# The last pair of row tiles: one finished earlier and normalized by ScalarE, the other's last product in two pieces, with bn_stats, stored by halves

## The chip, the cores and the metric

The kernel runs on one core of a Trainium2 chip. The core has a matrix engine (TensorE, PE in the profile; its weight loads are PEld), a vector engine (VectorE, DVE), an activation engine (ScalarE, ACT), a general engine (GpSimd, POOL), and SyncE (SP), which here issues nearly all transfers between the chip's memory (HBM) and the core's SBUF. Matrix products go to PSUM, from where VectorE or ScalarE fetch them. The metric is the device time of one execution in microseconds (us). The engines run in parallel and wait for each other through semaphores.

## The reference

All arrays are float32. x has 4 x 512 rows of 1024. The two layers, cut to what matters:

```python
attn = einsum('ds,td->st', w1, w2) * sparse_mask          # (1024, 1024), a band
y    = gelu(einsum('bds,st->bdt', x, attn) + b2)          # exact gelu
x    = layernorm(x + y)                                   # eps 1e-5, over 1024
w_l  = table lookup of 4-bit codes; w_h = of 8-bit codes  # (1024, 1024) each
y    = where(norm(x) > 64, x @ w_h.T, x @ w_l.T) + bias
x    = layernorm(x + y)
```

The kernel computes with a banded mask and with w_l alone, counts the rows and mask columns for which that isn't enough, and branches at the end to a general path if there are any. There are none with these inputs, so the general path is jumped over.

## The kernel before

Rows are taken in NT = 16 row tiles of P = 128 rows; D = 1024, HALF = 512, KT = 8 blocks of 128 along the contraction, EARLY = 4, PAIR = 2. The first layer and the unpacking of the codes come first; the second layer follows. w_l.T + I stands in SBUF as wT (the I adds the residual x). Row tiles 0 to 3 have the second layer by plain products (`ffn_half`). Row tiles 4 to 15 have it in six pairs (`ffn_pair(pool, n, blocks, between)`), by a scheme that needs seven products of half size instead of eight: the two row tiles' inputs in halves of the contraction are a11, a12 (row tile n) and a21, a22 (row tile n+1), their sums and differences are s1 to s4, the weight's quarters are b11, b12, b21, b22, and differences of them t1 to t4. The seven products of a pair go into three PSUM buffers of 512 columns, u, v and w; each is a call of `times`, which makes four matmuls of 128 x 512, and a float32 matmul shows as two instructions in the profile, so eight per product. In the program's order:

- u = a11*b11; DVE writes y11 = u + bias (line 642)
- w = s1*t1; y22 = w + bias (line 646)
- u += s2*t2; y12 = u + bias (line 649)
- w += s4*b22; row tile n's right half is w + y12 (line 651)
- u += s3*t3; row tile n+1's right half is u + y22 (line 653)
- v = a12*b21; row tile n's left half is v + y11 (line 656), and row tile n is finished
- u += a22*t4; row tile n+1's left half is u + bias (line 659), and row tile n+1 is finished

`combine` (line 522) is the addition on DVE that writes the result into x_tiles and sums it over its columns into `sums`. `finish_rows` (line 534) adds the two sums (line 537), and `stats` (line 347) makes the negative mean (line 351), lets ACT square and sum the centred row (line 354), and POOL turn that into one over the standard deviation r (lines 356 and 357). The last step, `normalize` on DVE (line 361) and the store by SP (line 546), is put on a list, `later`, which `now()` works off: for row tile n after the pair's last `combine` (line 660), for row tile n+1 in the next pair (line 643), or, in the last pair, at line 759.

DVE executes in the order in which the program is written (line 715). The other engines' order is made by a planner from the program's order and an estimate of the time: in the last pair it put the first half of v's eight matmuls ahead of s2*t2, and the other half behind s3*t3. POOL prepares s2 and s4 of a pair (lines 615 and 616). SP's transfers inside the pairs (lines 583, 589) reorder the next pair's rows; the last pair has none. After the pairs every engine loads the count of exceptions (line 762), and branches (line 763). At the end SP passes a row of semaphores and all engines meet in a barrier (line 798).

The buffers that the change touches: `work` tag "z" (two buffers, outputs o of row tiles from 4 on), `last` tag "o" (outputs of row tiles 0 to 3), `b2_bc` (the first layer's bias in all partitions, last read in the first layer), `bias_bc`.

Of the kernel before, what the change touches and what calls it, by code (L numbers as in the profile page):

```python
# [9 lines left out]
FP = mybir.dt.float32  # L10
# [3 lines left out]
AF = mybir.ActivationFunctionType  # L14
ALU = mybir.AluOpType
AX = mybir.AxisListType

P = 128
D = 1024
SOON = 12  # L20
PAIR = 2
KT = D // P
HALF = 512
NH = D // HALF
EPS = 1e-5
# [167 lines left out]
def kernel(  # L193
# [13 lines left out]
    nc = tc.nc  # L207
    x = x.flatten_outer_dims()
    out = out.flatten_outer_dims()
    NT = x.shape[0] // P  # L210
# [4 lines left out]
    with ExitStack() as main:  # L215
# [9 lines left out]
        work = main.enter_context(tc.tile_pool(name="work", bufs=1))  # L225
# [21 lines left out]
        minus_half = const.tile([P, 1], FP, name="minus_half")  # L247
# [3 lines left out]
        b2_bc = const.tile([P, D], FP, name="b2_bc")  # L251
        bias_bc = const.tile([P, D], FP, name="bias_bc")
# [94 lines left out]
        def stats(u, total):  # L347


            nm = work.tile([P, 1], FP, tag="nm", name="nm", bufs=4)  # L350
            nc.vector.tensor_scalar(nm, total, -1.0 / D, None, ALU.mult)  # L351
            junk = work.tile([P, D], BF, tag="junk", name="junk", bufs=1)
            ss = work.tile([P, 1], FP, tag="ss", name="ss", bufs=4)
            nc.scalar.activation(junk, u, AF.Square, bias=nm, accum_out=ss)  # L354
            r = work.tile([P, 1], FP, tag="r", name="r", bufs=4)
            nc.gpsimd.tensor_scalar(r, ss, 1.0 / D, EPS, ALU.mult, ALU.add)  # L356
            nc.gpsimd.tensor_tensor(r, r, minus_half, ALU.pow)  # L357
            return nm, r, ss

        def normalize(dst, u, nm, r):  # L360
            nc.vector.tensor_scalar(dst, u, nm, r, ALU.add, ALU.mult)  # L361

        x_tiles = []
# [9 lines left out]
        with tc.tile_pool(name="prod", bufs=1) as prod:  # L373
# [41 lines left out]
            for s in range(KT):  # L415
# [4 lines left out]
                for k in range(KT):  # L420
                    nc.tensor.matmul(  # L421
                        out=ps[:, : hi - lo],
                        lhsT=w1_sb[s][:, k, :],
                        rhs=w2T[:, k, lo:hi],
                        start=(k == 0),
                        stop=(k == KT - 1),
# [55 lines left out]
        def now():  # L482
            while later:
                later.pop(0)()
# [35 lines left out]
        sums = const.tile([P, NT, NH], FP, name="sums")  # L520

        def combine(n, h, ps, other):

            return nc.vector.scalar_tensor_tensor(  # L524
                x_tiles[n][:, ts(h, HALF)],
                ps,
                1.0,
                other,
                ALU.mult,
                ALU.add,  # L530
                accum_out=sums[:, n, h : h + 1],
            )

        def finish_rows(n):
            y = x_tiles[n]
            total = work.tile([P, 1], FP, tag="total", name="total", bufs=4)
            nc.vector.tensor_tensor(total, sums[:, n, 0:1], sums[:, n, 1:2], ALU.add)
            nm, r, _ = stats(y, total)

            def rest():  # L540
                if n < EARLY:
                    o = last.tile([P, D], FP, tag="o", name="o")
                else:
                    o = work.tile([P, D], FP, tag="z", name="o", bufs=2)
                normalize(o, y, nm, r)
                nc.sync.dma_start(out=out[ts(n, P), :], in_=o)

            later.append(rest)
# [14 lines left out]
        b21, b22 = wT[:, KH:, :HALF], wT[:, KH:, HALF:]  # L563
# [55 lines left out]
        def ffn_pair(pool, n, blocks, between):  # L619

            a11, a12, a22, s1, s2, s3, s4 = blocks
            t1, t2, t3, t4 = (weights[i] for i in range(1, 5))
            u = pool.tile([P, HALF], FP, tag="u", name="u", bufs=2)
            v = pool.tile([P, HALF], FP, tag="v", name="v", bufs=1)
            w = pool.tile([P, HALF], FP, tag="w", name="w", bufs=1)

            def times(ps, a, b, start, stop):
                for k in range(KH):
                    nc.tensor.matmul(  # L629
                        out=ps,  # L630
                        lhsT=a[:, k, :],
                        rhs=b[:, k, :],
                        start=start and k == 0,
                        stop=stop and k == KH - 1,
                        skip_group_check=True,
                    )

            left, right = bias_bc[:, :HALF], bias_bc[:, HALF:]
            y11, y12 = x_tiles[n][:, :HALF], x_tiles[n][:, HALF:]
            y22 = x_tiles[n + 1][:, HALF:]  # L640
            times(u, a11, b11, True, False)
            nc.vector.tensor_tensor(y11, u, left, ALU.add)
            now()
            between(0)
            times(w, s1, t1, True, False)
            nc.vector.tensor_tensor(y22, w, right, ALU.add)
            between(1)
            times(u, s2, t2, False, False)
            nc.vector.tensor_tensor(y12, u, right, ALU.add)  # L649
            times(w, s4, b22, False, True)  # L650
            combine(n, 1, w, y12)
            times(u, s3, t3, False, False)
            combine(n + 1, 1, u, y22)
            between(2)
            times(v, a12, b21, True, True)
            combine(n, 0, v, y11)
            finish_rows(n)
            times(u, a22, t4, False, True)
            combine(n + 1, 0, u, left)
            now()  # L660
            finish_rows(n + 1)

        def count_odd():


            nc.vector.tensor_scalar(ssq, ssq, EST_T * EST_T, None, ALU.is_gt)
            nc.vector.tensor_scalar(outside, outside, 0.0, None, ALU.is_equal)
            nc.vector.tensor_scalar(outside, outside, -1.0, 1.0, ALU.mult, ALU.add)
            n_odd = const.tile([P, 1], FP, name="n_odd")
            nc.vector.tensor_reduce(n_odd, odd, AX.X, ALU.add)  # L670
            return n_odd
# [39 lines left out]
        for i, (what, n) in enumerate(todo):  # L711
# [4 lines left out]
            if (what, n) == ("attention", SOON - 2):  # L716
# [3 lines left out]
                last = main.enter_context(tc.tile_pool(name="last", bufs=1, side="right"))  # L720
# [32 lines left out]
        for n in range(EARLY, NT, PAIR):  # L753
            ffn_pair(ps_pair, n, blocks[n], lambda part, m=n + PAIR: prepare_pair(m, part))
            if n == EARLY:
                n_odd = count_odd()
            elif n == EARLY + PAIR:
                count_all(n_odd)
# [44 lines left out]
```

## Time and profile before

| what | us |
|---|---|
| median of three runs (366.29 to 367.3) | 366.83 |
| the profiled execution | 366.59 |
| its span, first to last instruction | 364.7 |
| TensorE busy in the span | 328.5 (90%) |
| VectorE busy | 231.1 (63%) |
| ScalarE busy | 166.3 (46%) |
| GpSimd busy | 83.5 (23%) |
| last product of the last pair on TensorE | 350.02 to 353.62 |
| start of the last normalization on VectorE | 357.71 |
| issue of the last store by SyncE | 358.55 |

The mean granted TensorE clock of this execution is 0.966 of full speed. Times inside the execution count from the start of its span. A row of the profile names the line, the engine, the operation, what it writes and reads with the shapes, and how often; a "q" behind an engine's name (SPq, ACTq) means the engine's instruction queue, which waits, branches and issues transfers while the engine itself may still be busy. A span's end is not its time: 1.9 us of the profiled execution lie outside its span.

### The profile page before, as it was taken

How to read it: one execution, taken by the hardware profiler on the slowest of the kernel's cores; microseconds unless marked ns; L12 is line 12 of the kernel's file. 1: busy time of each engine (PE TensorE's matmuls, PEld its weight loads, DVE VectorE, ACT ScalarE, POOL GpSimd, SP SyncE). 2: the span in 40 equal slices, each digit the busy share in tenths (PEclk: the TensorE clock that was granted, in tenths of full speed). 3: DMA queues.
4: the chain of work that ended last, by engine and by line, in shares of the span. 5: the costliest groups of instructions: out<-in, count | busy, mean ns of one | idle time of the engine just before them, and what ended most of it. 6: DMA issues, size and time to landing. Idle time of an engine off the chain costs nothing.

```text
span 364.7 us, 3670 instructions
## 1 busy us (share of the span) xinstructions
PE 328.5 (90%) x1202; PEld 202.1 (55%) x1202; DVE 231.1 (63%) x351; ACT 166.3 (46%) x242; POOL 83.5 (23%) x130
## 2 busy tenths in 40 slices
PE   4599977989999997999999888999999999999970
PEld 3488866876566586866665433443444444444430
DVE  2589887887988997367676854564635526634130
ACT  0994983989649975675444411301212112012011
POOL 0600420454054111212312440401203004013000
PEclk9699998999999999699999999999999999999995
DMA  9997407700011000812154315143251451432003
GB/s 224 333 373 238 162 2 290 286 2 0 3 46 43 0 3 6 309 44 100 39 176 158 120 58 173 58 177 112 115 180 50 175 170 58 173 117 115 1 4 121
DMA packets 28347, 43.90 MB, mean 120 GB/s; under 512 B 7584, under 2 KB 20640, under 8 KB 28320
## 3 DMA queue, kind: packets, MB, share of 16 engines
q1 hardware_dynamic: 23056, 43.00, 33.3%
q10 hardware_dynamic: 5264, 0.59, 1.2%
q8 instruction: 11, 0.18, 0.2%
q14 instruction: 16, 0.13, 0.1%
HBM read 28.90 MB, written 14.68 MB: 119 GB/s over the span
## 4 chain that ended last, share of the span: by engine, by line
PE 34%; DVE 27%; ACT 16%; issue 8%; DMA 6%; POOL 5%; SPq 1%; ACTq 1%; POOLq 0%; DVEq 0%
PE u L629 16%; PE w L629 8%; ACT junk L354 7%; DVE x L498 5%; PE v L629 4%; DMA rows<-there 3%; DVE e L310 3%; PE mm L467 3%; ACT e L303 3%; DVE z L493 3%; POOL r L357 2%; POOL r L356 2%; DVE root L312 2%; DVE root L311 2%; ACT z L494 2%
## 5 line engine op out<-in xcount | busy, mean ns | idle before, releaser
L354 ACT ACTIVATE junk<-x,nm 128x1024 bf16<-128x1024 f32 x32 | 36.8, 1148 | 66.2 <-DVE nm L351 63.9
L467 PE MATMUL mm<-attn,xT 128*128 128x198 f32 (+2 forms) x320 | 63.7, 357 | 3.0 <-ACT xT L264 3.0
L467 PEld LDWEIGHTS mm<-attn,xT 128*128 128x128 f32 x320 | 55.6, 200 | 10.4 <-ACT xT L264 3.2
L303 ACT ACTIVATE e<-v,lt,diff 128x1024 f32<-128x1024 uint8 x48 | 56.7, 1238 | 6.1 <-DVE v L278 6.1
L512 PE MATMUL mm<-wT,xT 128*128 128x512 f32 x128 | 56.5, 594 | 0.6 <-DVE x L524 0.6
L629 PE MATMUL u<-t,halves 128*128 128x512 f32 x96 | 43.3, 594 | 1.0 <-DVE x L649 1.0
L356 POOL TENSOR_SCALAR r<-ss 128x1 f32<-128x1 f32 x32 | 11.5, 359 | 123.9 <-ACT junk L354 123.9
L512 PEld LDWEIGHTS mm<-wT,xT 128*128 128x128 f32 x128 | 23.7, 190 | 27.7 <-issue 27.4
L307 POOL TENSOR_SCALAR root<-v,diff,lt 128x1024 f32<-128x1024 uint8 x16 | 24.3, 1524 | 58.6 <-DVE v L278 44.0
L629 PEld LDWEIGHTS u<-t,halves 128*128 128x128 f32 x96 | 18.1, 190 | 24.6 <-issue 22.8
L611 ACT COPY halves<-rows 128x1024 f32<-128x1024 f32 x6 | 6.3, 1042 | 55.6 <-DMA rows<-there 55.6
L579 DVE STREAM_TRANSPOSE squares<-x 128x1024 f32<-128x1024 f32 x12 | 24.3, 2026 | 11.5 <-DMA there<-squares 11.5
L421 PE MATMUL mm<-w2T,w_sb 128*128 128x268 f32 (+1 forms) x128 | 30.0, 391 | 0.0
L615 POOL TENSOR_TENSOR halves<-halves 128x512 f32<-128x512 f32 x6 | 9.5, 1584 | 85.4 <-DVE halves L612 85.4
L263 PE MATMUL pt<-ident,x 128*128 128x128 f32 x160 | 22.4, 284 | 7.0 <-ACT wT L264 6.4
L421 PEld LDWEIGHTS mm<-w2T,w_sb 128*128 128x128 f32 x128 | 24.9, 203 | 3.1
L361 DVE TENSOR_SCALAR x<-x,nm,r 128x1024 f32<-128x1024 f32 x16 | 13.0, 812 | 20.4 <-POOL r L357 15.8
L311 DVE COPY_PREDICATED root<-v,e 128x1024 f32<-128x1024 uint8 x16 | 22.5, 1405 | 5.3 <-ACT e L303 4.0
L264 ACT COPY xT<-pt 128x512 f32<-128x512 f32 x40 | 21.0, 585 | 10.3 <-PE pt L263 7.2
L498 DVE SCALAR_TENSOR_TENSOR x<-z,x 128x1024 f32<-128x1024 f32 x16 | 21.5, 1342 | 5.3 <-ACT z L494 5.3
L263 PEld LDWEIGHTS pt<-ident,x 128*128 128x128 f32 x160 | 19.2, 155 | 10.0 <-ACT wT L264 7.8
L494 ACT ACTIVATE z<-z 128x1024 f32<-128x1024 f32 x16 | 16.9, 1054 | 15.8 <-DVE z L493 15.8
(71 smaller groups left out, 434.3 us busy)
## 6 DMA issues: line engine op xcount, KB each, us to landing
x<-in_L_attn_x_dram SPq DMA_DIRECT2D x16, 512.0 KB, 6.5
out_dram<-o SPq DMA_DIRECT2D x16, 512.0 KB, 2.6
there<-squares SPq DMA_DIRECT2D x12, 512.0 KB, 3.0
rows<-there SPq DMA_DIRECT2D x48, 128.0 KB, 2.9
w_raw<-in_L_attn_w_dram SPq DMA_DIRECT2D x8, 512.0 KB, 5.2
w_sb<-in_L_attn_w_dram SPq DMA_DIRECT2D x3, 1024.0 KB, 7.4
w_sb<-in_L_attn_w_dram SPq DMA_DIRECT2D x2, 512.0 KB, 4.9
raw<-_L_attn_sparse_mask_dram SPq DMA_DIRECT2D x2, 413.0 KB, 3.3
```

The costliest lines, as they stand in the source:

```text
L263: nc.tensor.transpose(pt[:, j, :], block(g * (HALF // P) + j), ident)
L303: nc.scalar.activation(entry[j], plane(0), AF.Identity, scale=d_k, bias=l_k)
L307: nc.gpsimd.tensor_scalar(entry[j], plane(0), d_k, l_k, ALU.mult, ALU.add)
L311: nc.vector.copy_predicated(root, plane(1), entry[1])
L354: nc.scalar.activation(junk, u, AF.Square, bias=nm, accum_out=ss)
L421: nc.tensor.matmul(out=ps[:, : hi - lo], lhsT=w1_sb[s][:, k, :], rhs=w2T[:, k, lo:hi], start=(k == 0), stop=(k == KT - 1),)
L467: nc.tensor.matmul(out=ps[:, a:b], lhsT=xT[:, s, :], rhs=attn[:, s, a - lo : b - lo], start=h not in fresh, stop=hi == D or (h == 0 and wi ...
L494: nc.scalar.activation(z, z, AF.Gelu)
L498: nc.vector.scalar_tensor_tensor(xt, z, 1.0, xt, ALU.mult, ALU.add, accum_out=total)
L512: nc.tensor.matmul(out=ps, lhsT=xT[:, k, :], rhs=wT[:, k, ts(h, HALF)], start=(k == 0), stop=(k == KT - 1),)
L579: nc.vector.transpose(out=t, in_=x_tiles[n].rearrange("t (c j k) -> t c k j", c=Q, k=KT))
L629: nc.tensor.matmul(out=ps, lhsT=a[:, k, :], rhs=b[:, k, :], start=start and k == 0, stop=stop and k == KH - 1, skip_group_check=True,)
```

## The change

In the last pair (n + PAIR == NT) the product v = a12*b21 stands ahead of s3*t3. Row tile n is then complete, and a new function finishes it: its statistics as before, then POOL multiplies the negative mean by r, ACT normalizes (Identity with a scale and a bias per row) and issues the store itself, from `last` tag "o".

For row tile n+1, s3*t3 closes u. DVE adds u to y22 (the right half) and the bias to u (the left half, without its last product). The last product, a22*t4, goes into w in two pieces of 256 columns; each is added to the left half as soon as it is there. The row's mean and variance come from bn_stats on four pieces of 256 columns and bn_aggr, with their small outputs in b2_bc; DVE adds eps, POOL raises to the power -0.5, DVE normalizes by halves, and the halves are stored by SP and by ACT.

```diff
@@ ffn_pair
             times(w, s4, b22, False, True)
             combine(n, 1, w, y12)
+            if n + PAIR == NT:
+                times(v, a12, b21, True, True)
+                combine(n, 0, v, y11)
+                finish_last(pool, n, lambda: times(u, s3, t3, False, True), u, w, a22, t4, y22)
+                return
             times(u, s3, t3, False, False)
@@ after ffn_pair
+        def finish_last(pool, n, third, u, w, a22, t4, y22):
+            total = work.tile([P, 1], FP, tag="total", name="total", bufs=4)
+            nc.vector.tensor_tensor(total, sums[:, n, 0:1], sums[:, n, 1:2], ALU.add)
+            nm, r, _ = stats(x_tiles[n], total)
+            nc.gpsimd.tensor_tensor(nm, nm, r, ALU.mult)
+            o = last.tile([P, D], FP, tag="o", name="o")
+            nc.scalar.activation(o, x_tiles[n], AF.Identity, scale=r, bias=nm)
+            nc.scalar.dma_start(out=out[ts(n, P), :], in_=o)
+
+            third()
+            y = x_tiles[n + 1]
+            pieces = 4
+            piece = D // pieces
+
+            n_st = pieces * nc.vector.BN_STATS_DIM
+            st = b2_bc[:, :n_st].rearrange("p (c f) -> p c f", c=pieces)
+            mv = b2_bc[:, n_st : n_st + 2]
+
+            def statistics(c):
+                nc.vector.bn_stats(st[:, c, :], y[:, ts(c, piece)])
+
+            nc.vector.tensor_tensor(y22, u, y22, ALU.add)
+            nc.vector.tensor_tensor(y[:, :HALF], u, bias_bc[:, :HALF], ALU.add)
+            for c in (2, 3):
+                statistics(c)
+            for c in (0, 1):
+                for k in range(KT // 2):
+                    nc.tensor.matmul(
+                        out=w[:, ts(c, piece)],
+                        lhsT=a22[:, k, :],
+                        rhs=t4[:, k, ts(c, piece)],
+                        start=(k == 0),
+                        stop=(k == KT // 2 - 1),
+                        skip_group_check=True,
+                    )
+                nc.vector.tensor_tensor(
+                    y[:, ts(c, piece)], w[:, ts(c, piece)], y[:, ts(c, piece)], ALU.add
+                )
+                statistics(c)
+            nc.vector.bn_aggr(mv, st)
+            r = work.tile([P, 1], FP, tag="r", name="r", bufs=4)
+            nc.vector.tensor_scalar(r, mv[:, 1:2], EPS, None, ALU.add)
+            nc.gpsimd.tensor_tensor(r, r, minus_half, ALU.pow)
+            o = work.tile([P, D], FP, tag="z", name="o", bufs=2)
+            for h, queue in ((0, nc.sync), (1, nc.scalar)):
+                nc.vector.tensor_scalar(
+                    o[:, ts(h, HALF)],
+                    y[:, ts(h, HALF)],
+                    mv[:, 0:1],
+                    r,
+                    ALU.subtract,
+                    ALU.mult,
+                )
+                queue.dma_start(out=out[ts(n + 1, P), ts(h, HALF)], in_=o[:, ts(h, HALF)])
```

## The prediction

> **What bounds the kernel now.** I read the page first, then the chain of waits over the last pair of row tiles, then the end in order of time, then the queue instructions of the program's last lines. TensorE works through the last pair without a gap, and the chain says so: it runs on PE from 329.58 to 353.63, through VectorE, ScalarE and GpSimd to the last normalization, and no transfer is in it.
>
> ```profile
> 341.60 3.43 PE w L629 x8
> 345.03 3.43 PE u L629 x8
> 348.47 1.72 PE v L629 x4
> 350.18 3.45 PE u L629 x8
> ...
> 353.65 0.07 DVE x L524
> ...
> 354.36 0.73 DVE o L361
> ...
> 355.52 0.74 ACT junk L354
> ...
> 357.71 0.81 DVE o L361
> ```
>
> The reader is to see two stretches: the last product (350.18 to 353.63), and 4.9 us of small dependent steps behind it, with the 0.73 us of the other row tile's normalization among them. What follows is not a transfer either. These are the rows of line 763 (the branch over the general path, and what each engine does behind it), and of the last stores:
>
> ```profile
> L763 SPq EVENT_SEMAPHORE  x8: 17/17/17, 362.5 to 363.0; - x8
> ...
> L763 ACTq COMPARE_BRANCH  x1: 50/50/50, 356.3 to 356.3; - x1
> ...
> L763 DVEq COMPARE_BRANCH  x1: 72/72/72, 358.3 to 358.3; - x1
> ...
> L763 SPq COMPARE_BRANCH  x1: 45/45/45, 358.9 to 358.9; - x1
> L763 ACTq EVENT_SEMAPHORE  x1: 17/17/17, 359.0 to 359.0; - x1
> L763 DVEq EVENT_SEMAPHORE  x1: 21/21/21, 361.6 to 361.6; - x1
> ```
>
> ```profile
> L546 SPq DMA_DIRECT2D out_dram<-o x2: 332/332/332, 355.1 to 358.5; - x2
> ...
> DMA to landing us min/median/max: 2.6/3.1/3.5
> ```
>
> SP issues the last store at 358.55 and branches at 358.93; its next instruction comes at 362.52, 3.54 us after the branch. The same gap is 2.64 us on ACT (356.38 to 359.02) and 3.15 on DVE (358.42 to 361.56). Then SP passes 20 semaphores until 363.86, and a barrier ends the span at 364.69. The store has landed by 362.1, so it is hidden. The end is therefore "issue of SP's last store plus 6.14 us", and what the change is worth is how much earlier SP issues its last store.
>
> By the Trainium skill, page "Runtime: NRT & Kernel Launch", section "Instruction fetch mechanics", a taken branch whose target lies outside the two pages held waits for a DMA that fetches it. SP's 3.54 us agree, and by that rule ACT, which now issues the very last store, pays a gap of its own behind it.
>
> **Part 1: row tile n finished early, by ACT.** Product v now stands before the product s3*t3. The six products up to there are the same 48 matmuls, 0.429 apart, so s3*t3 still ends at 350.18 and v at 346.75. Row n then goes: combine 346.8 to 347.5, sum and mean to 347.9, Square 1.15 and its read 0.19 to 349.3, POOL's two operations 0.19 and 0.55 to 350.2, the added POOL product 0.2 to 0.55 (lines 504, 505), ACT's Identity 1.15 to 1.24 (lines 354, 303), to 352.0, and the store's issue on ACT's queue, 0.33 (SP's) to 0.57 (median of line 235). It lands about 355.4, before the next store starts. ACT has nothing else from 333.5 on; behind that store only the last half store waits. SP has one store fewer. All this lies beside TensorE's work and costs nothing; without that cover Identity and issue would cost 1.7. Gained on the path: the 0.73 of normalization at 354.36.
>
> **Part 2: the last product in two pieces.** Sixteen matmuls of 256 columns replace eight of 512. Sixteen matmuls of 268 columns of line 421 start from 43.1 to 46.5, 0.227 apart, fifteen of 198 from 46.9 to 49.3, 0.168 apart; 256 lies at 0.216, so TensorE needs 16 x 0.216 = 3.45 instead of 3.43, no loss. A matmul's record ends 0.163 after the next may start (592 against 429 ns).
>
> VectorE, after s3*t3: y22 at 350.22 and the bias half at 350.83 (line 612 follows itself by 0.61), two bn_stats, the first add. The trace has no bn_stats; bounds for 256 elements are 0.285 (line 278, 128x256) and 0.51 (a quarter of line 579's 2.03, VectorE's slowest pass). I take 0.36, between 0.285 and the 0.42 of a two-input operation, with steps of 0.30. So the first add is at 352.04, while piece 0 is out at 350.02 + 7 x 0.216 + 0.38 = 351.91. The add takes 0.42 (line 428: 0.356 for 198 columns, 0.430 for 268), to 352.46.
>
> Now the added wait. Both pieces lie in one buffer, w, and in program order the read of the first stands before the matmuls of the second. Whether TensorE waits for a read of other columns of its buffer no row shows. Lower end: no wait, piece 1 out at 350.02 + 15 x 0.216 + 0.38 = 353.64. Upper end: it waits, as it does for a read of the same columns:
>
> ```profile
> 220.79 0.65 DVE L649 TENSOR_TENSOR x<-u,bias_bc 128x512 f32<-128x512 f32 x1
> ...
> 221.50 1.55 PE L629 MATMUL u<-t,halves 128*128 128x512 f32 x3 [1.02 <-DVE x L649]
> ```
>
> There the read ended at 221.44, TensorE started 0.05 later and its second matmul came 0.10 late. So piece 1 starts at 352.51 and is out at 352.51 + 0.10 + 7 x 0.216 + 0.38 = 354.50, 0.86 later. I take the upper end: the nearest row is a PSUM buffer read by DVE and written again by PE, and that row waits. Queued behind the waiting matmul are the other 15 and PE's own branch, which has 5 us to spare.
>
> The Trainium skill, page "PSUM — Partial Sum Buffer", section "Terms", says that a bank is 2 KiB of a partition and that TensorE and VectorE in one bank at the same time is an error. By that rule the wait must be there, since w's 512 f32 are one bank, and the time is 365.2; without it 364.3. No run here shows it.
>
> **Part 3: the tail of row n+1.** From the second add, 0.04 after the piece: add 0.42, bn_stats 0.36, bn_aggr 0.18 (line 670 has 0.186 for 32 elements; 0.15 to 0.41, by 128x1 and 128x128), epsilon 0.15 (line 351), POOL's power 0.55 behind a hop of 0.10, hop back 0.04, first half of the normalization 0.46 (between 285 ns at 256 and 812 at 1024 columns; 0.41 to 0.69), three gaps of 0.04 between dependent VectorE steps, 0.03 to the issue. Sum 0.42 + 0.36 + 0.18 + 0.15 + 0.65 + 0.04 + 0.46 + 0.12 + 0.03 = 2.41, where before 353.62 to 358.55 were 4.93. Gone with Square, its read, POOL's scaling and the sum: 2.5 us.
>
> **Part 4: halves on two queues.** SP issues the first half at 354.54 + 2.41 = 356.95 and is done. ACT issues the second 0.38 later, at 357.3, in 0.33 to 0.57; its load of the count (0.70, line 762) may stand behind it; branch 0.05; gap 2.64 to 3.54: ACT is back by 361.0 to 362.2. SP's last semaphore is passed at 356.95 + 5.31 = 362.26. So ACT is hidden, by as little as 0.1. The second half lands 2.6 to 3.5 after its issue, by 360.8, also hidden. Nothing is gained by the halves but the shorter first operation, 0.35, already in the 0.46. SP's own gap, 3.54, is bounded by ACT's 2.64 and by 4.4, if a third engine's overlapping gap costs SP as much as the second did (0.9); I keep 3.54.
>
> **Sum.** 356.95 - 358.55 = -1.6: span 363.1. The profiled execution took 366.59 for its 364.7, so 365.0; it is 0.24 under the median 366.83, so 365.2 for a median. Bounds: bn_stats counts twice before the first add and once after (-0.2, +0.55), aggregate and half +0.3, SP's gap -0.9 to +0.9. Not all fall together: the forecast's own range is 364.6 to 366.2.
>
> **Rivals.** *No wait between the pieces*: -2.5, 364.3. For it: the columns are disjoint, and for SBUF a disjoint range is no reason to wait: a load into other columns of raw was issued at 170.8 while the work on its first columns began at 172.5. Against: the row of line 649.
>
> *bn_stats is slow*: at 0.9 us for 256 elements the three that count cost 1.6 more and nothing is gained, 366.8. Against: that is nearly twice VectorE's slowest pass.
>
> *The change doesn't do what it says*: TensorE's order is the planner's. Before, half of v (336.29, four matmuls) was put ahead of a product that stands earlier in the program. Were piece 0 put ahead of s3*t3, that product would end at 351.9, the first add at 354.2, piece 1 at 356.2 and the store at 358.6: 366.8. Against: s3*t3 waits for nothing late, its last reader of u being done at 342.3.
>
> *The gaps behind the branch are served one after another* (the other side): DVE, SP and ACT now branch within 1 us. Three gaps of 2.64 in turn from 357.1 end at 365.0 on ACT, and the barrier's 0.83 makes 365.9: +1.2, 368.1. It decides once ACT's gap passes 5.2 us. For it: SP's 3.54 beside DVE's. Against: those two overlapped by 2.6 us and were only 0.5 and 0.9 longer than ACT's alone.
>
> **How the numbers follow.** 0.3% is 1.1 us, about what a measurement of this kernel can tell. Forecast 0.58, no wait 0.19, slow bn_stats 0.08, other order 0.06, gaps in turn 0.09. Faster: 0.51 of the forecast and the 0.19, 0.70. Same: 0.07 of the forecast, most of the slow bn_stats, the other order, 0.19. Slower: the gaps in turn and the worse end of bn_stats, 0.11. Range 364.0 to 367.0: it leaves out the gaps in turn, the fast end of no wait and the slow tails, under 0.2.
>
> **What would show it.** A gap of TensorE of about 0.8 us before the second piece, released by VectorE's first add; without one, the first rival. Row n's store issued near 352; SP's last store near 356.95 and the span's end 6.1 behind it; ACT's first instruction behind its branch before SP's. The prediction is wrong if SP's gap grows past 4.4, or if the first add comes much later than 352.0.

## The result

The changed kernel takes 365.17 us (median of 20 runs, 364.11 to 366.56) where the kernel before takes 366.41 (median of 20, 365.51 to 367.67): ratio 0.9967, 95% interval 0.9956 to 0.9978, or 1.2 us less. The forecast was 365.2, from a gain of 1.6; so the time came out as said, and the gain smaller by a quarter. That the time agrees to 0.03 us is luck: the kernel before measured 0.4 lower here than the 366.83 from which the forecast started, and the gain came out smaller by as much. A second set, on another occasion, gave 0.9964 (0.9945 to 0.9983).

The work ahead of the last product takes 348.8 to 350.4 us in the traces, with no edit there that would explain it. Traces are therefore compared below by the time since the six products of the last pair were done (350.02 in the profiled execution before, 349.89 in that after). From there to the span's end it is 14.70 before and 13.27 after.

### The profile page after: what moved, and what is told of

The parts are those of the page before. It is cut to its first block, busy times and chain, and to the rows that moved or that the text cites. A ratio compares the mean times of both kernels' runs of the same rounds, so it can differ in the third digit from the quotient of the medians.

```text
span 363.2 us, 3688 instructions
## 1 busy us (share of the span) xinstructions
PE 328.7 (91%) x1210; PEld 203.4 (56%) x1210; DVE 234.0 (64%) x355; ACT 166.4 (46%) x241; POOL 84.9 (23%) x130
## 4 chain that ended last, share of the span: by engine, by line
PE 34%; DVE 28%; ACT 15%; issue 7%; POOL 5%; DMA 5%; ACTq 2%; SPq 1%; POOLq 0%; DVEq 0%
PE u L629 15%; PE w L629 8%; ACT junk L354 6%; DVE x L498 5%; PE v L629 4%; DVE e L310 4%; DMA rows<-there 3%; PE mm L467 3%; ACT e L303 3%; DVE z L493 3%; POOL r L357 2%; POOL r L356 2%; DVE root L312 2%; DVE root L311 2%; ACT z L494 2%
## 5 line engine op out<-in xcount | busy, mean ns | idle before, releaser
L354 ACT ACTIVATE junk<-x,nm 128x1024 bf16<-128x1024 f32 x31 | 35.6, 1149 | 60.4 <-DVE nm L351 58.1
L307 POOL TENSOR_SCALAR root<-v,diff,lt 128x1024 f32<-128x1024 uint8 x16 | 23.1, 1453 | 60.7 <-DVE v L278 46.1
L310 DVE COPY_PREDICATED e<-v,e 128x1024 f32<-128x1024 uint8 x16 | 23.3, 1456 | 1.3 <-ACT e L303 1.3
```

What stands on the lines that cost most here:

```text
L307: nc.gpsimd.tensor_scalar(entry[j], plane(0), d_k, l_k, ALU.mult, ALU.add)
L310: nc.vector.copy_predicated(entry[2], plane(1), entry[3])
```

## The profile after

The chain of waits of the changed kernel over the last pair (start, us, what):

```profile
346.62 3.45 PE u L629 x8
...
350.09 0.69 DVE x L691
350.78 0.60 DVE x L692
...
351.63 0.41 DVE b_bc L689
352.04 0.33 DVE x L705
...
352.41 2.01 PE w L697 x8
...
354.45 0.44 DVE x L705
...
354.91 0.44 DVE b_bc L689
...
355.37 0.28 DVE b_bc L709
...
356.48 1.00 DVE o L715 x2
```

Square, its read and row tile n's normalization are gone from the tail. But TensorE is on the chain in the middle of VectorE's steps: its second piece (line 697, from 352.41) follows VectorE's first add. In order of time:

```profile
351.96 0.40 DVE L705 TENSOR_TENSOR x<-w,x 128x256 f32<-128x256 f32 x1
...
352.41 1.99 PE L697 MATMUL w<-t,a 128*128 128x256 f32 x8 [0.64 <-DVE x L705]
```

The add ends at 352.36 and the second piece starts 0.05 later, 0.64 us after TensorE ran idle. The rows of the branch (line 825 here) and of the last half stores (line 723):

```profile
L825 SPq EVENT_SEMAPHORE  x8: 17/17/17, 360.3 to 361.5; - x8
...
L825 SPq COMPARE_BRANCH  x1: 45/45/45, 357.4 to 357.4; - x1
...
L825 ACTq EVENT_SEMAPHORE  x1: 17/17/17, 361.4 to 361.4; - x1
```

```profile
L723 SPq DMA_DIRECT2D out_dram<-o x1: 333/333/333, 357.1 to 357.1; - x1
L723 ACTq DMA_DIRECT2D out_dram<-o x1: 362/362/362, 357.5 to 357.5; - x1
...
DMA to landing us min/median/max: 3.5/3.5/3.6
```

SP's gap behind its branch is 2.82 us, not 3.54; its eight semaphores, which took 0.5 before (362.5 to 363.0), now take 1.2. The third is passed at 361.14, just behind the landing of ACT's half at 361.12. The last store is no longer hidden.

## The experiments

All ratios are to the kernel before, measured beside it on the same chip. "Since the six" is the trace's measure from above; its three columns are the issue of SP's last store, the last landing, and the span's end. They come from one execution each; the two kernels that were traced twice (e9 repeats the changed kernel, e10 repeats e2) agree to 0.01 us at the issue and to 0.04 and 0.23 at the end.

| kernel | ratio (95%) | SP's issue | landing | end |
|---|---|---|---|---|
| before | 1 | 8.53 | 12.05 | 14.70 |
| e5, row tile n early, rest as before | 0.9982 (0.9968, 0.9996) | 7.85 | 11.15 | 13.98 |
| e6, and bn_stats | 0.9963 (0.9949, 0.9977) | 7.10 | 10.68 | 13.23 |
| e4, and halves | 0.9944 (0.9921, 0.9966) | 6.83 | 10.43 | 12.48 |
| changed: and two pieces | 0.9967 (0.9956, 0.9978) | 7.17 | 11.23 | 13.27 |
| e2, and two PSUM buffers | 0.9936 (0.9914, 0.9957) | 6.26 | 9.86 | 11.90 |
| e3, the changed kernel with one store | 0.9978 (0.9957, 1.0) | 7.44 | 11.52 | 13.65 |
| e9, the changed kernel again | 0.9964 (0.9945, 0.9983) | 7.16 | 11.47 | 13.50 |
| e10, two PSUM buffers again | 0.9935 (0.992, 0.995) | 6.26 | 9.90 | 11.94 |

**Row tile n alone, first try (e1).** Row tile n early and by ACT; the last product goes on in u, and all of row tile n+1 as before.

```diff
-            times(u, s3, t3, False, True) ... bn_stats, pieces, halves
+            times(u, s3, t3, False, False)
+            combine(n + 1, 1, u, y22)
+            times(u, a22, t4, False, True)
+            combine(n + 1, 0, u, bias_bc[:, :HALF])
+            finish_rows(n + 1)
```

> Only the first part of the change: v is taken before s3*t3, row tile n is finished early and normalized and stored by ACT; row tile n+1 is computed and finished as in the kernel before. Theory (the gain is the sum of several savings in the tail, less a wait of TensorE): only the 0.73 us of row tile n's normalization leaves the path, so the time is 0.5 to 0.9 us below the kernel before (ratio 0.9975 to 0.9986). Rival A (row tile n's early finish is the whole gain, the rest cancels itself): 1.1 to 1.5 below, ratio about 0.9967. Rival B (nothing on the path but the statistics): no change.

Measured: 366.62, ratio 1.0017 (1.0002 to 1.0033). All three missed: it is not faster, if anything slower. The timeline says why:

```profile
349.85 0.69 DVE L524 SCALAR_TENSOR_TENSOR x<-u,x 128x512 f32<-128x512 f32 x1 [2.28 <-PE u L629]
...
350.70 3.67 PE L629 MATMUL u<-t,a 128*128 128x512 f32 x8 [0.88 <-DVE x L524]
```

VectorE reads u after s3*t3, and the last product writes u. In the kernel before, half of v stood between the two and covered that read; with v taken earlier the cover is gone, and TensorE's start comes 1.05 late (350.70, against 349.22 + 0.43).

**Row tile n alone, into w (e5).** The same, with the bias added to u's left half on VectorE, and the last product into w.

```diff
             combine(n + 1, 1, u, y22)
-            times(u, a22, t4, False, True)
-            combine(n + 1, 0, u, bias_bc[:, :HALF])
+            nc.vector.tensor_tensor(y21, u, bias_bc[:, :HALF], ALU.add)
+            times(w, a22, t4, True, True)
+            combine(n + 1, 0, w, y21)
```

> The first part of the change again, now with the last product taken whole into w, as the change takes it, so that it doesn't write the buffer u that VectorE has still to read; row tile n+1 keeps the old statistics and one store. Theory (in the first try TensorE stood 1.05 us because the last product went on in u, and that hid the saving): no such pause, SP's last store is issued 0.6 to 0.8 us sooner against the last of the six products than in the kernel before, and the time is 0.5 to 0.9 below the kernel before, ratio 0.9975 to 0.9986. Rival (row tile n's normalization was not on the path, or ACT's work on row tile n delays row tile n+1): no pause and still no gain, ratio 0.999 to 1.001.

Measured: 365.64, ratio 0.9982, no pause, SP's issue 0.68 sooner since the six. The theory holds: the first part is worth the 0.73 us that the normalization held in the chain, if the last product leaves u.

**bn_stats, one store (e6); halves, one piece (e4); one store, two pieces (e3).** e6 takes the last product whole and stores once; e4 takes it whole and stores by halves; e3 is the changed kernel with one store.

```diff
 # e3 and e6, instead of the loop over halves
+            nc.vector.tensor_scalar(o, y, mv[:, 0:1], r, ALU.subtract, ALU.mult)
+            nc.sync.dma_start(out=out[ts(n + 1, P), :], in_=o)
 # e4 and e6, instead of the loop over pieces
+            for k in range(KT // 2):
+                nc.tensor.matmul(out=w, lhsT=a22[:, k, :], rhs=t4[:, k, :], ...)
+            nc.vector.tensor_tensor(y[:, :HALF], w, y[:, :HALF], ALU.add)
+            for c in (0, 1):
+                statistics(c)
```

> Row tile n early, the last product whole in w, bn_stats and bn_aggr, but one normalization of 1024 columns and one store by SP. Against the run before it, it adds bn_stats alone; against e4 it lacks the halves alone. Theory: bn_stats replaces sum, mean, Square, its read and POOL's scaling and saves 0.6 to 0.8 on the path, so the time is 1.2 to 1.6 below the kernel before (ratio 0.9956 to 0.9967); SP's gap behind its branch is near 3.5, as in all kernels with one last store of 512 KB, and the halves of e4 are worth the other 0.7 to 1.0. Rival (SP's gap differs from run to run and has nothing to do with the halves): the gap is near 2.85 here too, and the ratio is e4's, 0.994.

> The changed kernel with the last product in one piece of 512 columns, one add and then the two bn_stats behind it. Theory (the wait between the pieces eats what they save): the product ends at 353.5 in the changed kernel's time instead of 354.4; the add takes 0.2 more and one more bn_stats step of 0.33 stands behind it, so the last bn_stats ends 0.2 to 0.4 sooner than with two pieces: 0.1 to 0.4 faster than the changed kernel, ratio 0.9955 to 0.9965. Rival (the pieces pay, because the first add and its statistics are hidden): 0.3 to 0.6 slower than the changed kernel, ratio 0.9975 to 0.9985.

> The changed kernel with row tile n+1 normalized in one operation and stored by SP alone, in one transfer. Theory (the halves are worth nothing, since the changed kernel's end waits for the landing of the second half, 3.6 us after its issue): SP issues 0.27 us later than in the changed kernel, but the one transfer starts 0.2 sooner than the second half did and ACT no longer branches late; the end is the changed kernel's within 0.3, ratio 0.9963 to 0.9973. Rival (the halves carry part of the gain, as SP's issue of the first half starts the end): 0.3 to 0.7 slower than the changed kernel, ratio 0.9975 to 0.9986.

Measured: e6 364.78 (0.9963); e4 363.75 (0.9944); e3 365.33, ratio 0.9978 (0.9957 to 1.0). bn_stats are worth 0.75 at SP's issue (7.85 to 7.10), as said. The halves bring SP's issue 0.27 sooner, and SP's gap with them 2.88 instead of 3.50:

```profile
L815 SPq EVENT_SEMAPHORE  x8: 17/17/17, 360.2 to 360.7; - x8
...
L815 SPq COMPARE_BRANCH  x1: 45/45/45, 356.7 to 356.7; - x1
```

```profile
L823 SPq EVENT_SEMAPHORE  x8: 17/17/17, 359.5 to 360.2; - x8
...
L823 SPq COMPARE_BRANCH  x1: 45/45/45, 356.6 to 356.6; - x1
```

The first is e6, the second e4: the branches come 0.05 apart, the next instructions 0.67. Over all kernels with the branch the gap is 3.50 to 3.54 with one store of 512 KB (five kernels) and 2.82 to 3.08 with halves (eight executions). So e3's theory, that halves are worth nothing, does not hold: its end comes 0.38 later than the changed kernel's since the six, and the ratio is its rival's, though the interval covers the theory's too. For e4 the theory's side is right and its size too small: one piece is faster than the change's two in one buffer, 12.48 against 13.27 since the six. Of these 0.79, 0.34 lie at SP's issue, as the theory said; the rest goes with the landing of ACT's half, 3.14 after its issue instead of 3.60, which is taken up below. The pieces, as the change makes them, are a loss by the traces; the intervals of the two ratios overlap.

**Two buffers (e2, e10).** The second piece into v, which is free by then.

```diff
+            into = (w[:, :piece], v[:, :piece])
             for c in (0, 1):
                 for k in range(KT // 2):
                     nc.tensor.matmul(
-                        out=w[:, ts(c, piece)],
+                        out=into[c],
```

> The changed kernel with its second piece in the free PSUM buffer v instead of the other columns of w. Theory (TensorE waits because both pieces share a PSUM buffer): TensorE goes on at 351.6 instead of 352.4, the second add starts 0.77 us sooner, and the time is 0.6 to 0.8 below the changed kernel, 1.8 to 2.1 below the kernel before (ratio 0.9943 to 0.9952). Rival (TensorE's pause comes from the order of the work or from VectorE being late, not from the shared buffer): the pause stays and the ratio is the changed kernel's 0.9967. Rival (the end is set by something else, as the landing of row tile n+1 stores or ACT's branch): the pause goes and less than 0.3 us comes of it.

> The changed kernel itself, beside the others on one chip. Theory: its pause of TensorE is 0.8 us again (the matmul before it starts 1.01 before the one behind it, instead of 0.216), TensorE resumes behind its branch about 357, its 16 KB fetch falls into the last stores, and the second half lands 3.5 to 4.4 after its issue; ratio 0.9956 to 0.9978. Rival (the late landing was an accident of one execution): landing near 3.14 with the same pause.

> The kernel with two PSUM buffers again, on the same chip as the changed kernel. Theory: 0.9 us sooner by the pause and 0.3 to 0.5 by the landing, 1.1 to 1.5 below the changed kernel: ratio to the kernel before 0.992 to 0.9945. Rival (the first chip flattered it): 0.995 to 0.997.

Measured: e2 363.45, ratio 0.9936; on one chip, the changed kernel (e9) 365.08, 0.9964 (0.9945 to 0.9983), and two buffers (e10) 363.85, 0.9935 (0.992 to 0.995). The timeline of e2:

```profile
350.52 1.89 PE L698 MATMUL v<-t,a 128*128 128x256 f32 x8
...
350.86 0.41 DVE L706 TENSOR_TENSOR x<-w,x 128x256 f32<-128x256 f32 x1
...
352.45 0.42 DVE L706 TENSOR_TENSOR x<-v,x 128x256 f32<-128x256 f32 x1 [0.72 <-PE v L698]
```

TensorE now writes v before and while VectorE reads w, with no idle time. So it was the shared buffer that held it, worth 0.91 at SP's issue (7.17 to 6.26). But the end comes 1.37 sooner (1.56 from e9 to e10). The other 0.46 (0.66) goes with the landing: ACT's half takes 3.14 and 3.18 from its issue in the two executions with two buffers, 3.60 and 3.85 in the two of the changed kernel. What differs there is shown by the transfers of the last 7 us, first of the changed kernel, then of e10 ("instruction" are the engines' own fetches of instructions; packets, MB, share):

```profile
q14 instruction: 7, 0.06, 2.8%
q8 instruction: 1, 0.02, 1.2%
```

```profile
q14 instruction: 7, 0.06, 2.3%
```

One 16 KB packet on queue 8, at 357.63 and 1.36 us long, runs in the changed kernel while the halves are stored (in e9 at 358.81). It comes 0.6 behind TensorE's first instruction after its own branch (357.03); with two buffers TensorE is there at 352.45 and 353.70, before the stores. TensorE's queue shows as PEldq; first the changed kernel, then e2:

```profile
L825 PEldq COMPARE_BRANCH  x1: 3362/3362/3362, 353.6 to 353.6; - x1
...
L825 PEldq EVENT_SEMAPHORE  x1: 51/51/51, 357.0 to 357.0; - x1
```

```profile
L826 PEldq COMPARE_BRANCH  x1: 3522/3522/3522, 348.5 to 348.5; - x1
L826 PEldq EVENT_SEMAPHORE  x1: 51/51/51, 352.5 to 352.5; - x1
```

**TensorE late, with two buffers (e7).** One more product behind the last piece.

```diff
                 statistics(c)
+            times(u, a22, t4, True, True)
             nc.vector.bn_aggr(mv, st)
```

> The kernel with two PSUM buffers, and behind its last product one more product of 512 columns into u that nobody reads: TensorE is done 3.4 us later, at about 355.8 in that kernel's time, and nothing waits for it but the end of the program. Theory (TensorE's instruction fetch behind its branch, 16 KB in one packet, falls into the last stores and delays their landing): the fetch now lies between 356 and 358, the second half lands 3.5 to 3.7 after its issue instead of 3.14, and SP waits for it; the time is 0.3 to 0.6 above the kernel with two buffers. Rival (the landing differs from run to run, or only TensorE's pause counts): landing near 3.14 and the ratio of the kernel with two buffers, 0.9936, within its interval.

Measured: 365.07, ratio 0.9963 (0.9947 to 0.9978); SP's issue at 6.26 as in e2, the 16 KB packet at 358.21, 1.61 us long, and

```profile
q8 instruction: 1, 0.02, 1.5%
```

```profile
DMA to landing us min/median/max: 3.1/3.8/4.4
```

instead of e2's 3.1/3.2/3.2: ACT's half lands 4.42 after its issue. The theory holds, with a larger size than said: product and fetch cost 1.28 since the six, with every engine's work on the last rows unchanged. The work that TensorE had left is read by nobody.

**No branch (e8).** The kernel before, without lines 762 to 764.

> The kernel before without the load of the count, the branch and the general path behind it (the part that would run for exceptional rows or masks is left out). Theory (the branch gap of SP, 3.5 us, hides the landing of the last store, and the landing is next): SP comes to its semaphores at once, waits for the store, which lands 2.6 to 3.5 after its issue, and the end comes 0.5 to 1.5 earlier: ratio 0.996 to 0.9986. Rival (the landing or the barrier sets the end in the kernel before, the gap is hidden): no change, within 0.1%.

Measured: 363.34, ratio 0.9927 (0.9906 to 0.9949), 2.6 since the six, beyond the theory's range. Its last store and SP's wait for it:

```profile
DMA to landing us min/median/max: 2.6/2.6/2.6
```

```profile
L794 SPq EVENT_SEMAPHORE  x7: 17/28/2162, 357.9 to 361.1; - x7
```

The store lands 2.58 after its issue instead of 3.52, and from the landing to the end it is 1.0 instead of 2.65: SP needn't come back first, which in the kernel before it did 0.45 behind the landing (362.07 to 362.52), and it has 5 semaphores to pass in all and not 20. 0.94 + 1.65 = 2.6. So the gap hid a landing that was itself 0.94 longer with the branch. That the instruction fetches behind the branch lengthen it is the likely reading, since without them it is 2.58; no run has these fetches alone.

**Three pieces (e11); both halves by SP (e12).** e11 takes 256, 128 and 128 columns in w, v and u; e12 is e2 with both stores on SP's queue.

```diff
 # e11
+            cuts = (0, 256, 384, 512, 768, 1024)
+            for c, ps in enumerate((w, v, u)):
+                a, b = cuts[c], cuts[c + 1]
 # e12
-            for h, queue in ((0, nc.sync), (1, nc.scalar)):
+            for h, queue in ((0, nc.sync), (1, nc.sync)):
```

> Three pieces of 256, 128 and 128 columns in the three PSUM buffers w, v and u, five bn_stats. Theory (behind TensorE's end only the last piece's add and statistics stand, and they scale with its columns): add 0.29 and bn_stats 0.29 instead of 0.42 and 0.43, the aggregate 0.03 more; SP's store 0.2 to 0.3 sooner against the end of the six products than with two buffers and two pieces, ratio 0.9985 to 1.0 of that kernel's. Rival (matmuls of 128 columns cost more than half of those of 256, as a weight load of 0.19 stands before each): TensorE ends up to 1.3 us later (16 matmuls at 0.19 instead of 0.109) and the kernel is 0.5 to 1.1 slower than with two pieces.

> The kernel with two PSUM buffers, and both halves issued by SP. Theory (the end is SP's last issue, its gap and the landing): SP issues 0.46 later and branches 0.46 later, the second half lands as before; SP's way through its semaphores starts 0.3 to 0.5 later, 0.2 to 0.5 slower than with two queues. Rival (two queues or ACT's late branch cost something, three fetches at a time): SP's gap gets shorter by as much, no difference within 0.1 us in the span behind the last issue; second rival (SP's gap goes back to 3.5, as with one store of 512 KB on its queue): 1.0 to 1.3 slower.

Measured: e11 364.33, ratio 0.9958 (0.994 to 0.9976); e12 364.20, 0.9941 (0.9923 to 0.9959). In e11 matmuls of 128 columns start 0.111 apart, so its rival's dear matmuls are refuted, and SP's issue is 0.18 sooner (6.08). Still the end comes at 13.20: TensorE takes its branch 2.15 after the six (351.43) instead of 0.25 before (e10, 349.79), comes back at 356.22, its 16 KB packet runs at 357.59, and ACT's half lands 4.62 after its issue. Neither theory had that; it is the changed kernel's second loss again. The third piece goes into u: VectorE's last read of u ends at 350.77, and TensorE's load of the count, which stands ahead of its branch, starts at 350.84. e7, which also writes u again, has the same 0.07 (351.69 to 351.76), and in both the branch takes 4.73 us instead of 3.4 to 4.0 in the other kernels; why, stays open. e12 ends 0.6 later than e2 since the six, just beyond its theory's 0.5; the ratio's difference is within the intervals. SP's gap is 2.95 there, so 512 KB on SP's queue by themselves do not make it 3.5.

## Why the prediction was right, point by point

- **Part 1** (0.73 gained, all beside TensorE): right. ACT's Identity took 1.24, row n's store was issued at 351.65 (said 352.0), and e5 shows 0.68. That the last product must leave u for it wasn't said; e1 shows 1.05 lost without.
- **Part 2, the added wait**: right in kind and size. Since the six, the first add came at 2.07 (said 2.02), the second piece at 2.52 (2.49), the second add at 4.56 (4.52); e2 shows that the shared buffer is the cause. By the Trainium skill, page "PSUM — Partial Sum Buffer", section "Terms", two engines may not be in one bank at once; the trace agrees as far as it goes, with the pause at 0.64 idle when both pieces lie in w's 2 KB and none when they lie in two buffers. What the trace shows is a wait for a semaphore; what would come without it, no run shows.
- **The bn_stats bounds**: 0.41 to 0.43 for 256 elements where 0.36 was taken; bn_aggr 0.26 for 0.18, each half of the normalization 0.55 for 0.46. The tail took 2.65 from TensorE's end to SP's issue, against 2.45: the term that was mis-sized, 0.2.
- **SP's gap** (3.54 kept): wrong by 0.7, and so "nothing is gained by the halves but the shorter first operation". They bring the gap to 2.82; e4 and e6 show it.
- **The second half's landing** ("by 360.8, also hidden"): wrong. It landed at 361.12 and SP waited for it, which gave back 0.65 of the shorter gap. The step that failed is the one on TensorE's branch, "which has 5 us to spare": its gap has, but its fetch then meets the stores. Even without that meeting the landing isn't hidden behind the shorter gap: in e2 SP's third semaphore is passed at 358.67, 0.25 behind the second instead of 0.08, with the landing at 358.65. The two errors cancel, by luck: 6.10 from SP's issue to the end, against 6.14 said. One sign named beforehand failed with the gap: ACT's first instruction behind its branch came at 361.43, after SP's at 360.31 and not before.
- **The rivals.** No wait: refuted by the trace, and its price, 0.9, was short by 0.46 (0.66 by e9 and e10), as the wait also moves TensorE's fetch. Slow bn_stats and another order of TensorE: didn't happen. Gaps in turn: refuted, DVE's, SP's and ACT's gaps of 3.5, 2.8 and 2.6 overlapped (its sum, 366.83 + 1.2, gives 368.0, not 368.1).

So the forecast of 1.6 stood 0.2 too high by the new operations in the tail; the rest of the difference from the measured 1.2 is within the interval (0.8 to 1.6).

## What to carry to other kernels

Splitting a product to hide its evacuation paid here only with the pieces in different PSUM buffers; in one, the second piece waits for the read of the first. Since the six, two pieces in one buffer ended at 13.27, one piece at 12.48, two buffers at 11.90. The ratios have the same order (0.9967, 0.9944, 0.9936), but their intervals overlap, so the small step from one piece to two buffers rests on the traces. When a product is moved, ask which reader of its neighbour's buffer it covered. At a program's end, look behind the last store: a branch, the instruction fetches that it sets off on all engines and the landing of the store hang together, and an engine whose work nobody waits for any more can delay the end.

## What the hardware showed that was not expected

- An instruction fetch of 16 KB during the last stores went with a landing 0.5 to 1.5 us later: for the second half 3.60, 3.85, 4.42 and 4.62 with it, 3.11 to 3.18 without; for one store 4.09 (e3) with it, 3.30 to 3.58 without; 2.58 with no fetch at all (e8). In e7 the edit alone put the fetch there.
- The packets show that such a fetch holds up a part of a store. Each store goes as 128 packets. In e1 the 16 KB packet of TensorE's branch (352.24 to 353.85) fell into row tile n's store, with no other fetch near: 120 packets were through by 353.71, the last eight ran one after another from 353.83 to 355.48, and the store landed 4.55 after its issue, against 2.67 in the changed kernel and in e5. In e7 and e11 the last eight packets of ACT's half start at 359.79 and 359.01, where the 16 KB packet ends at 359.82 and 359.03. Eight of 128 is the share of one of the 16 transfer engines; the trace doesn't name the engine of a packet, so that these eight shared one with the fetch is inferred from the times.
- SP's gap behind its branch was 0.4 to 0.7 shorter when the last 512 KB went as halves (packets of 2 KB, 84 ns, instead of 4 KB, 159 ns), also with both on one queue. VectorE's gap grew meanwhile, 3.22 to 3.54 from e6 to e4. Whether the packets' size or the first store's length does it stays open; a whole store in packets of 2 KB wasn't tried. SP's branch also follows VectorE's by 0.32 to 0.33 in the kernels with halves on two queues and by 0.59 in those with one store; e12, with 0.98 and a gap of 2.95, speaks against a simple order of turns.
